# A selective-scan layer stage: a quarter of the B products on GpSimd, the skip term as a diagonal matmul, the gate on VectorE

## The chip, the cores and the metric

The kernel runs on one NeuronCore of a Trainium2 chip. The metric is the device time of one launch in microseconds, a median over runs. A core has a matrix engine (TensorE, in the profile PE, its weight loads PEld), three engines for elementwise work (VectorE = DVE, ScalarE = ACT, GpSimd = POOL) and SyncE (SP), which here only issues transfers. Each engine takes its instructions in the order in which they were written; they wait for one another by semaphores. TensorE writes to PSUM (eight banks of 128 x 512 fp32), the other data lie in SBUF.

## The reference

The network has four layers on an image x of shape (2, 128, 64, 64). Only the first, two rounds of a selective state-space block, is touched by the change. With `t` the tokens (2 images x 4096 positions, 128 channels), each round computes:

```python
xz = layernorm(t) @ in_w.T                     # u and z: 256 channels each
u  = silu(causal_conv4(u) + conv_b)
dt, Bm, Cm = split(u @ xproj_w.T, [8, 24])     # 8, 16 and 16 columns
dt = softplus(dt @ dt_w.T + dt_b)
dA = exp(dt[..., None] * A);  dBu = (dt * u)[..., None] * Bm[:, :, None, :]
h  = dA_t * h + dBu_t                          # scan over 4096 positions, 256 x 16 states
y  = einsum('bdn,bn->bd', h, C_t)
y  = (y + u * ssm_D) * silu(z)
t  = t + y @ out_w.T
t  = t + gelu(layernorm(t) @ w1.T + b1) @ w2.T + b2
```

Before the rounds stands a 1x1 embedding, behind them a 1x1 output projection and a residual. The later layers (two attention layers over 4096 positions, and a multi-scale layer) follow.

## The kernel before

The layer stage works on items: one image, one round, one chunk of CH = 512 positions, so 2 x 2 x 8 = 32 items. The states of an item are 256 channels x 16. They are laid out as NST = 8 groups; a group holds 32 channels x 4 state quarters on the 128 partitions, and in the free dimension m = 4 states of 512 positions. So one item has 32 slots, each one scan instruction of 128 x 512: slot t belongs to group g = t // 4, state m = t % 4.

All is written in one loop over slots, by hand; the order on each engine is the order written. For each slot the loop gives, in this order:

- at m = 0: `spread_dt` (SyncE copies 32 rows of dt to the four quarters of `dtb`, four transfers, for a group two ahead), `spread_dtu` (a TensorE matmul with a selection matrix puts dt*u of the next group on all quarters, into the PSUM tile `pdu`, which has one bank), and in odd groups `y_pair` (eight TensorE matmuls with a 128 x 32 selection sum h*C of two groups over the states into `py`, one bank);
- `scan` (VectorE, line 358): h = da * h + h along 512 positions, starting from `carry`. After m = 3 GpSimd saves the last column (line 360) and multiplies the group by C (line 361, 2048 elements a partition);
- `decay` (ScalarE, line 347): da = exp(A * dtb) for the slot four ahead, into one of four PSUM banks;
- at m = 3: `times_b` (VectorE, line 340): h of the next group = B * pdu, 2048 elements a partition;
- the background work of that slot, from a table in `background(i)`.

The background table spreads over the 32 slots of item i what its neighbours need: the item before it (p = i - 1) is finished, the next one (n = i + 1) gets its projections, i + 2 its first layer norm. The entries that matter here, by slot:

- 0 to 6: the convolution and z projections (`pu_taps`, `pz_mm`, each matmul followed by a ScalarE copy), gelu of item i - 2 (slot 3), `y_out` and `gate` of p (slot 6: VectorE forms y + D*u from PSUM, line 381; GpSimd multiplies by z, line 384), the second feed-forward matmuls (6 and 7);
- 8: `mix_out` (three matmuls, lines 390 and 391), 10: `mix_add` (ScalarE, line 394), 11: silu with two activation table loads;
- 12 to 15: layer-norm centring and squares; 13 and 14: `xproj` (B, C and the dt columns) and `spread_bc` (B and C go to DRAM, tile `dr`, and from there by eight transfers of 256 KB to `bb` and `cb`, two buffers each); 15 to 18: `dtproj`, softplus on ScalarE (line 315), `dt_end` (dt*u on GpSimd, line 321);
- 17 to 21: variance, inverse root, and one Newton step, `ln_newton` (line 226 on GpSimd, 227 on ScalarE) and `ln_step` (231 on GpSimd);
- 23: `y_out` of the item's first half; 27 to 29: the norm is spread (TensorE, line 235) and applied (VectorE, line 239); 30 and 31: the first feed-forward matmuls (line 403), into a tile `hid`.

The tiles h and hid rotate through one tag of five buffers. Small PSUM results share a tag of two banks, which ScalarE empties.

Of the kernel before, what the change touches and what calls it, by code (L numbers as in the profile page):

```python
# [6 lines left out]
F32 = mybir.dt.float32  # L7
AF = mybir.ActivationFunctionType
ALU = mybir.AluOpType
# [6 lines left out]
P = 128  # L16
CH = 512
# [3 lines left out]
DS = 16  # L21
DI = 2 * C
NJ = DI // P
R = (C + 15) // 16
NX = R + 2 * DS
KC = 4
# [41 lines left out]
def tile_conv_seq(ctx: ExitStack, tc, x, consts, vecs, wemb, wlay, wconv, wdt, wqkv, wsmall, wms, out):  # L68
# [30 lines left out]
    def v1(name, i=0):  # L99
        return vec[:, VEC[name] + i : VEC[name] + i + 1]  # L100
# [7 lines left out]
    with ExitStack() as s, tc.manual_schedule():  # L108
# [24 lines left out]
        wl, wu, wd, am = [], [], [], []  # L133
        for l in range(NL):
            w = wp.tile([P, NWL - DI], F32, name=f"wl{l}")
            nc.sync.dma_start(w, wlay[l][:, DI:])
            cw = sp.tile([P, KC + 1, DI], F32, name="cw", tag="h", bufs=5)
# [12 lines left out]
            for g in range(4):  # L150
                pa = mm.tile([P, NJ, DS], F32, name="pa", tag="mm")
                nc.tensor.matmul(pa.rearrange("p j n -> p (j n)"), lhsT=four(g), rhs=an, start=True, stop=True)
                for q in range(4):
                    at = slice(32 * q, 32 * q + 32)
                    nc.vector.tensor_copy(a[at, :, g, :], pa[at, :, 4 * q : 4 * q + 4])
            wl.append(w), wu.append(u), wd.append(d), am.append(a)
        for c in range(NCH):
            nc.sync.dma_start(xv(1, c), x[1, :, c * RPC : (c + 1) * RPC, :])
# [14 lines left out]
        def vl(name, i, k=0):  # L173
            return v1(f"{name}{items[i][1]}", k)
# [22 lines left out]

        def ln_square(w, k, i):
            if "sq" not in w:
                w["sq"] = sp.tile([P, 2, CH], F32, name="sq", tag="tmp", bufs=2)  # L200
# [39 lines left out]

        def ln_shift(w, k, i, second):
            if second:
                dst = st[i]["x2"] = sp.tile([P, CH], F32, name="x2", tag="tmp", bufs=2)
# [50 lines left out]
            st[i]["dbl"] = sp.tile([NX, CH], F32, name="dbl", tag="dbl")  # L294
            nc.scalar.copy(st[i]["dbl"], st[i].pop("pd"))

        def spread_bc(i):

            dr = dp.tile([2 * DS, CH], F32, name="dr", tag="dr")
            nc.sync.dma_start(dr, st[i]["dbl"][R:])  # L300
            for k in range(2):
                o = st[i]["bc", k] = sp.tile([P, 4, CH], F32, name=("bb", "cb")[k], tag=("bb", "cb")[k], bufs=2)
                for q in range(4):
                    src = dr[k * DS + 4 * q : k * DS + 4 * q + 4, :].rearrange("(o m) f -> o (m f)", o=1)
                    nc.sync.dma_start(o[32 * q : 32 * q + 32].rearrange("p m f -> p (m f)"), src.to_broadcast([32, 4 * CH]))

        def dtproj(i, j):
            st[i]["pt", j] = mmt("pt")
# [15 lines left out]
        def spread_dt(g):  # L324
            i, s_ = divmod(g, NST)
            o = st[i]["dtb", s_] = sp.tile([P, CH], F32, name="dtb", tag="dtb", bufs=4)
            k = 32 * (s_ % 4)
            for q in range(4):
                nc.sync.dma_start(o[32 * q : 32 * q + 32, :], st[i]["dt"][k : k + 32, s_ // 4, :])

        def spread_dtu(g):
            i, s_ = divmod(g, NST)
            pdu = st[i]["pdu", s_] = bc.tile([P, CH], F32, name="pdu", tag="bc")
            nc.tensor.matmul(pdu, lhsT=four(s_ % 4), rhs=st[i]["dtu"][:, s_ // 4, :], start=True, stop=True)  # L334

        def times_b(g):
            i, s_ = divmod(g, NST)
            h = st[i]["h", s_] = sp.tile([P, 4, CH], F32, name="h", tag="h", bufs=5)
            pdu = st[i].pop(("pdu", s_))
            nc.vector.tensor_tensor(h, st[i]["bc", 0], pdu.unsqueeze(1).to_broadcast([P, 4, CH]), ALU.mult)  # L340

        def decay(t):
            g, m = divmod(t, 4)
            i, s_ = divmod(g, NST)
            j, gg = divmod(s_, 4)
            da = st[i]["da", s_, m] = dap.tile([P, CH], F32, name="da", tag="da")
            nc.scalar.activation(da, st[i]["dtb", s_], AF.Exp, scale=am[items[i][1]][:, j, gg, m : m + 1])  # L347
# [15 lines left out]
        def y_pair(g):  # L363

            i, s_ = divmod(g, NST)
            j, gg = divmod(s_, 4)
            if gg == 0:
                st[i]["py", j] = yp.tile([P, CH], F32, name="py", tag="y")
            py = st[i]["py", j]
            for m in range(4):  # L370
                for k in range(2):
                    r = 32 * (gg + k)
                    nc.tensor.matmul(  # L373
                        py[r : r + 32, :], lhsT=sel, rhs=st[i]["h", s_ + k][:, m, :], start=(m == 0), stop=(m == 3),
                        tile_position=(0, r),
                    )


        def y_out(i, j):
            u = st[i]["u"][:, j, :]  # L380
            nc.vector.scalar_tensor_tensor(u, u, vl("ssm_D", i, j), st[i].pop(("py", j)), ALU.mult, ALU.add)

        def gate(i):
            nc.gpsimd.tensor_tensor(st[i]["z"], st[i]["z"], st[i]["u"], ALU.mult)

        def mix_out(i):
            po = st[i]["po"] = mmt("po")
# [9 lines left out]
        def ffn_up(i, f):  # L397
            w = st[i]
            if f == 0:
                w["hid"] = sp.tile([P, 4, CH], F32, name="hid", tag="h", bufs=5)  # L400
# [36 lines left out]
        def background(i):  # L437
# [3 lines left out]
            def at(t, f, *a):  # L441
                todo[t].append((f, a))
# [728 lines left out]
```

## Time and profile before

The time is 5351.36 us, the median of three runs (5349.31 to 5352.06). The profiled execution spans 5360.6 us.

| part of the span | us | what runs |
|---|---|---|
| layer stage, first to last scan | 83.5 to 2159.6 | 32 items of 32 slots |
| the layers behind it | to 5360.6 | attention and multi-scale layers |

| engine, whole span | busy us | share |
|---|---|---|
| PE | 4900.6 | 91% |
| DVE | 3798.2 | 71% |
| ACT | 2326.4 | 43% |
| POOL | 2287.5 | 43% |

How to read the profile: a group of instructions stands as line, engine, operation, output tile <- input tiles, shapes, count, then the busy time in us, the mean ns of one, and the idle time just before them with the instruction that ended most of it. A timeline line has the start, the length, the engine and the instruction, and in brackets the idle time before it with what ended it. In the list of waits, "A <- B: total, times, longest" says that A stood idle until B was done. One fp32 matmul shows as two records. Lines with "q" are the issuing of transfers or sequencer work.

### The profile page before, as it was taken

What the parts mean: (1) busy time and instruction counts of PE and PEld (TensorE: products, weight loads), DVE (VectorE), ACT (ScalarE), POOL (GpSimd) and SP (SyncE); (2) the same over time, 40 slices, a digit from 0 to 9 for tenths busy, and PEclk for the clock granted to TensorE, in tenths of its full rate; (3) what the DMA queues carried; (4) which work ended last, traced back from release to release, by engine and by line L of the source; (5) the groups of instructions that cost most, each with busy time, mean ns of one, the idle gap of its engine ahead of it and who ended that gap; (6) DMA issues with size and microseconds to landing.
All of it is one profiled execution on the core that took longest, in us unless ns stands there. A gap on an engine that the chain in (4) does not pass through costs nothing.

```text
span 5360.6 us, 48695 instructions
## 1 busy us (share of the span) xinstructions
PE 4900.6 (91%) x15085; PEld 2311.3 (43%) x15085; DVE 3798.2 (71%) x3810; ACT 2326.4 (43%) x2933; POOL 2287.5 (43%) x1948
## 2 busy tenths in 40 slices
PE   5888888888888898899999999999999998988997
PEld 1222222222222222356665566656666665333332
DVE  4998999889999999136663366667767775656665
ACT  4676777777777776212221122232323221223332
POOL 2766666666666767112221122223333332322221
PEclk8898889999898988899999999999999999999998
DMA  4222233222222232014442244444444442000000
GB/s 108 69 65 64 65 70 70 68 68 64 64 64 64 68 73 69 17 42 95 96 97 50 51 96 96 95 101 112 112 101 101 112 111 71 4 4 4 6 6 8
DMA packets 233843, 362.04 MB, mean 68 GB/s; under 512 B 87648, under 2 KB 88048, under 8 KB 225136
## 3 DMA queue, kind: packets, MB, share of 16 engines
q1 hardware_dynamic: 184432, 291.76, 23.2%
q10 hardware_dynamic: 49152, 67.17, 5.2%
q8 instruction: 121, 1.98, 0.2%
q14 instruction: 138, 1.13, 0.1%
HBM read 83.92 MB, written 6.29 MB: 17 GB/s over the span
## 4 chain that ended last, share of the span: by engine, by line
PE 59%; DVE 14%; DMA 10%; ACT 6%; SPq 4%; issue 4%; POOL 4%; ACTq 0%; DVEq 0%; POOLq 0%
PE pq L600 11%; PE po L647 11%; PE py L373 5%; PE pp L544 5%; DVE tr L627 4%; PE pu L262 4%; SPq L638 3%; DMA dtb<-dt 3%; DVE h L358 3%; DMA bb<-dr 3%; POOL h L361 3%; DMA pt<-tr 3%; PE pdu L334 2%; PE pf L861 2%; PE ph L403 2%
## 5 line engine op out<-in xcount | busy, mean ns | idle before, releaser
L634 POOL COPY pt<-tr 32x512 f32<-32x512 f32 x1024 | 628.0, 613 | 1680.7 <-DVE tr L627 911.8
L358 DVE TENSOR_TENSOR_SCAN h<-da,carry,h 128x512 f32<-128x512 f32 x1024 | 1240.2, 1267 | 97.6 <-ACT da L347 68.3
L361 POOL TENSOR_TENSOR h<-h,cb 128x2048 f32<-128x2048 f32 x256 | 1160.7, 4534 | 20.8 <-POOL carry L360 0.2
L604 DVE TENSOR_SCALAR_CACHE_REDUCE sc<-pq 128x1024 f32<-128x1024 f32 x512 | 625.9, 1223 | 760.6 <-PE pq L600 748.4
L647 PE MATMUL po<-pt,vt 128*128 128x256 f32 x4096 | 968.1, 380 | 4.8 <-DMA pt<-tr 4.8
L600 PE MATMUL pq<-k,q 128*128 128x512 f32 x2048 | 962.1, 592 | 4.8 <-ACT q L532 3.4
L647 PEld LDWEIGHTS po<-pt,vt 128*128 128x128 f32 x4096 | 776.4, 190 | 265.4 <-issue 170.6
L347 ACT ACTIVATE da<-dtb,am 128x512 f32<-128x512 f32 x1024 | 686.8, 685 | 390.3 <-DVE h L358 250.2
L613 ACT ACTIVATE sc<-sc,nm 128x4096 f32<-128x4096 f32 x128 | 474.8, 3709 | 721.9 <-DVE nm L611 615.6
L627 DVE STREAM_TRANSPOSE tr<-sc 128x2048 f32<-128x2048 f32 x256 | 589.3, 2302 | 37.9 <-DMA pt<-tr 24.5
L340 DVE TENSOR_TENSOR h<-bb,pdu 128x2048 f32<-128x2048 f32 x256 | 580.0, 2266 | 25.0 <-POOL carry L360 15.4
L373 PE MATMUL py<-h,sel 128*32 128x512 f32 x2048 | 506.7, 638 | 1.7 <-POOL h L361 1.7
L600 PEld LDWEIGHTS pq<-k,q 128*128 128x128 f32 x2048 | 383.5, 190 | 277.8 <-issue 248.7
L334 PE MATMUL pdu<-dtu,fsel 128*128 128x512 f32 x512 | 327.4, 726 | 87.8 <-DVE h L340 87.6
L532 ACT ACTIVATE q<-pqq,vec 128x256 f32<-128x256 f32 x64 | 30.4, 474 | 606.6 <-PE pqq L544 361.2
L373 PEld LDWEIGHTS py<-h,sel 128*32 128x32 f32 x2048 | 114.5, 117 | 412.5 <-issue 406.8
L544 PE MATMUL pp<-xt,wq 128*128 128x512 f32 x576 | 251.8, 598 | 6.6 <-DMA wq<-in_wqkv 6.2
L262 PE MATMUL pu<-xn,wu 128*128 128x512 f32 x512 | 246.1, 614 | 2.7 <-ACT xn L252 1.7
L235 PE MATMUL pr<-rs,kc 2*128 2x512 f32 (+1 forms) x128 | 117.1, 1059 | 133.1 <-POOL rs L231 126.9
L334 PEld LDWEIGHTS pdu<-dtu,fsel 128*128 128x128 f32 x512 | 95.2, 214 | 303.5 <-DVE h L340 187.9
L888 PE MATMUL pqkv<-f,ws 128*128 128x512 f32 x384 | 197.8, 641 | 10.2 <-ACT q L895 6.3
L950 DVE TENSOR_TENSOR ov<-v,pw 128x2048 f32<-128x2048 f32 x64 | 146.2, 2284 | 63.4 <-PE pw L943 63.3
(191 smaller groups left out, 5089.1 us busy)
## 6 DMA issues: line engine op xcount, KB each, us to landing
pt<-tr SPq DMA_DIRECT2D x2048, 64.0 KB, 2.0
dtb<-dt SPq DMA_DIRECT2D x1024, 64.0 KB, 2.0
pt<-tr ACTq DMA_DIRECT2D x1024, 64.0 KB, 2.1
bb<-dr SPq DMA_DIRECT2D x128, 256.0 KB, 4.5
cb<-dr SPq DMA_DIRECT2D x128, 256.0 KB, 7.6
xt<-in_x SPq DMA_DIRECT2D x16, 256.0 KB, 5.1
xr<-in_x SPq DMA_DIRECT2D x16, 256.0 KB, 3.1
out<-ot SPq DMA_DIRECT2D x16, 256.0 KB, 2.0
```

The costliest lines, as they stand in the source:

```text
L334: nc.tensor.matmul(pdu, lhsT=four(s_ % 4), rhs=st[i]["dtu"][:, s_ // 4, :], start=True, stop=True)
L340: nc.vector.tensor_tensor(h, st[i]["bc", 0], pdu.unsqueeze(1).to_broadcast([P, 4, CH]), ALU.mult)
L347: nc.scalar.activation(da, st[i]["dtb", s_], AF.Exp, scale=am[items[i][1]][:, j, gg, m : m + 1])
L358: nc.vector.tensor_tensor_scan(h[:, m, :], da, h[:, m, :], carries[b, l][:, j, gg, m : m + 1], ALU.mult, ALU.add)
L361: nc.gpsimd.tensor_tensor(h, h, st[i]["bc", 1], ALU.mult)
L373: nc.tensor.matmul(py[r : r + 32, :], lhsT=sel, rhs=st[i]["h", s_ + k][:, m, :], start=(m == 0), stop=(m == 3), tile_position=(0, r),)
L544: nc.tensor.matmul(ps, lhsT=wq[:, which, tap, :], rhs=rhs, start=(tap == 0), stop=(tap == 8))
L600: nc.tensor.matmul(pq[:, i, :], lhsT=st["q", r, grp][:, it * P : (it + 1) * P], rhs=st["k"][:, at : at + CH], start=True, stop=True)
L604: nc.vector.tensor_scalar(dst, pq, 1.0, None, ALU.mult, ALU.max, accum_out=st["mx"][:, c2 : c2 + 1])
L627: nc.vector.transpose(tr, half.rearrange("p (t r f) -> p r t f", r=NB, f=32))
L634: nc.gpsimd.tensor_copy(dst, src)
L647: nc.tensor.matmul(st["po", r, grp], lhsT=st["vt"][:, jt, :], rhs=rhs, start=(jt == 0), stop=(jt == N // P - 1))
```

## The change

It moves work of the scan loop among the engines, and reorders transfers:

- `times_b` keeps three of the four states on VectorE. The fourth is made by GpSimd (`times_b_last`, at m = 2, after the slot's background work). [...]ScalarE first copies pdu to SBUF (`copy_dtu`, at m = 1, tile `dub`, one buffer).
- The skip term D*u is no longer added by VectorE. A diagonal matrix `sd` of D, made in the setup, opens the accumulation of `py` with one more matmul for each half of an item.
- The gate, z*y, is one VectorE product that reads `py` from PSUM, for each half, at slots 7 and 23; the GpSimd product of the whole item goes. `mix_out` moves from slot 8 to 9.
- The transfers of C (slot 16) and of B (slot 27) are issued apart, and `bb` has one buffer in place of two; `spread_dt` runs three groups ahead in place of two.
- h and hid get six buffers in place of five; the tiles sq and x2 get a tag of their own.

```diff
-        def spread_bc(i):
-            for k in range(2):
-                o = st[i]["bc", k] = sp.tile([P, 4, CH], F32, name=("bb", "cb")[k], tag=("bb", "cb")[k], bufs=2)
+        def spread_bc(i, k):
+            o = st[i]["bc", k] = sp.tile([P, 4, CH], F32, name="bc"[k] + "b", tag="bc"[k] + "b", bufs=1 + k)
...
+        def copy_dtu(g):
+            o = st[i]["dub", s_] = sp.tile([P, CH], F32, name="dub", tag="dub")
+            nc.scalar.copy(o, st[i]["pdu", s_])
+        def times_b_last(g):
+            h = st[i]["h", s_] = sp.tile([P, 4, CH], F32, name="h", tag="h", bufs=6)
+            nc.gpsimd.tensor_tensor(h[:, 3, :], st[i]["bc", 0][:, 3, :], st[i].pop(("dub", s_)), ALU.mult)
         def times_b(g):
-            nc.vector.tensor_tensor(h, st[i]["bc", 0], pdu.unsqueeze(1).to_broadcast([P, 4, CH]), ALU.mult)
+            nc.vector.tensor_tensor(h[:, :3, :], st[i]["bc", 0][:, :3, :], pdu.unsqueeze(1).to_broadcast([P, 3, CH]), ALU.mult)
...
             if gg == 0:
-                st[i]["py", j] = yp.tile([P, CH], F32, name="py", tag="y")
+                py = st[i]["py", j] = yp.tile([P, CH], F32, name="py", tag="y")
+                nc.tensor.matmul(py, lhsT=skip[items[i][1]][:, j, :], rhs=st[i]["u"][:, j, :], start=True, stop=False)
...
-        def y_out(i, j):
-            nc.vector.scalar_tensor_tensor(u, u, vl("ssm_D", i, j), st[i].pop(("py", j)), ALU.mult, ALU.add)
-        def gate(i):
-            nc.gpsimd.tensor_tensor(st[i]["z"], st[i]["z"], st[i]["u"], ALU.mult)
+        def gate(i, j):
+            nc.vector.tensor_tensor(z, z, st[i].pop(("py", j)), ALU.mult)
...
-                at(6, y_out, p, 1), at(6, gate, p)
-                at(8, mix_out, p), at(10, mix_add, p)
+                at(7, gate, p, 1), at(9, mix_out, p), at(10, mix_add, p)
...
-                at(13, xproj, n), at(14, xproj_out, n), at(14, spread_bc, n)
+                at(13, xproj, n), at(14, xproj_out, n), at(14, store_bc, n), at(16, spread_bc, n, 1), at(27, spread_bc, n, 0)
...
-                at(23, y_out, i, 0)
+                at(23, gate, i, 0)
...
-                if m == 0 and 0 <= g + 2 < NG:
-                    spread_dt(g + 2)
+                if m == 0 and 0 <= g + 3 < NG:
+                    spread_dt(g + 3)
...
+                if m == 1 and 0 <= g + 1 < NG:
+                    copy_dtu(g + 1)
                 if m == 3 and 0 <= g + 1 < NG:
                     times_b(g + 1)
                 for f, a in todo[t_]:
                     f(*a)
+                if m == 2 and 0 <= g + 1 < NG:
+                    times_b_last(g + 1)
```

More of the change, by code (lines that the diff above doesn't have):

```diff
@@ L132, in tile_conv_seq @@
         nc.scalar.preload_act_table_set(EXP_LN_SET)
-        wl, wu, wd, am = [], [], [], []
+        wl, wu, wd, am, skip = [], [], [], [], []
         for l in range(NL):
@@ L136, in tile_conv_seq @@
             nc.sync.dma_start(w, wlay[l][:, DI:])
-            cw = sp.tile([P, KC + 1, DI], F32, name="cw", tag="h", bufs=5)
+            cw = sp.tile([P, KC + 1, DI], F32, name="cw", tag="h", bufs=6)
             nc.sync.dma_start(cw[:, :KC, :].rearrange("p k d -> p (k d)"), wconv[l : l + 1, :].to_broadcast([P, KC * DI]))
@@ L155, in tile_conv_seq @@
                     nc.vector.tensor_copy(a[at, :, g, :], pa[at, :, 4 * q : 4 * q + 4])
+            sd = wp.tile([P, NJ, P], F32, name=f"sd{l}")
+            for j in range(NJ):
+                nc.vector.tensor_scalar(sd[:, j, :], ident, v1(f"ssm_D{l}", j), None, ALU.mult)
+            skip.append(sd)
             wl.append(w), wu.append(u), wd.append(d), am.append(a)
@@ L199, in ln_square @@
             if "sq" not in w:
-                w["sq"] = sp.tile([P, 2, CH], F32, name="sq", tag="tmp", bufs=2)
+                w["sq"] = sp.tile([P, 2, CH], F32, name="sq", tag="sq")
                 w["cen"] = sp.tile([P, 2, CH], F32, name="cen", tag="cen")
@@ L242, in ln_shift @@
             if second:
-                dst = st[i]["x2"] = sp.tile([P, CH], F32, name="x2", tag="tmp", bufs=2)
+                dst = st[i]["x2"] = sp.tile([P, CH], F32, name="x2", tag="x2")
             else:
@@ L295, in xproj_out, with store_bc @@
             nc.scalar.copy(st[i]["dbl"], st[i].pop("pd"))
-        def spread_bc(i):
-            dr = dp.tile([2 * DS, CH], F32, name="dr", tag="dr")
-            nc.sync.dma_start(dr, st[i]["dbl"][R:])
-            for k in range(2):
-                o = st[i]["bc", k] = sp.tile([P, 4, CH], F32, name=("bb", "cb")[k], tag=("bb", "cb")[k], bufs=2)
-                for q in range(4):
-                    src = dr[k * DS + 4 * q : k * DS + 4 * q + 4, :].rearrange("(o m) f -> o (m f)", o=1)
-                    nc.sync.dma_start(o[32 * q : 32 * q + 32].rearrange("p m f -> p (m f)"), src.to_broadcast([32, 4 * CH]))
+        def store_bc(i):
+            st[i]["dr"] = dp.tile([2 * DS, CH], F32, name="dr", tag="dr")
+            nc.sync.dma_start(st[i]["dr"], st[i]["dbl"][R:])
+        def spread_bc(i, k):
+            o = st[i]["bc", k] = sp.tile([P, 4, CH], F32, name="bc"[k] + "b", tag="bc"[k] + "b", bufs=1 + k)
+            for q in range(4):
+                src = st[i]["dr"][k * DS + 4 * q : k * DS + 4 * q + 4, :].rearrange("(o m) f -> o (m f)", o=1)
+                nc.sync.dma_start(o[32 * q : 32 * q + 32].rearrange("p m f -> p (m f)"), src.to_broadcast([32, 4 * CH]))
         def dtproj(i, j):
@@ L334, in spread_dtu @@
             nc.tensor.matmul(pdu, lhsT=four(s_ % 4), rhs=st[i]["dtu"][:, s_ // 4, :], start=True, stop=True)
+        def copy_dtu(g):
+            i, s_ = divmod(g, NST)
+            o = st[i]["dub", s_] = sp.tile([P, CH], F32, name="dub", tag="dub")
+            nc.scalar.copy(o, st[i]["pdu", s_])
+        def times_b_last(g):
+            i, s_ = divmod(g, NST)
+            h = st[i]["h", s_] = sp.tile([P, 4, CH], F32, name="h", tag="h", bufs=6)
+            nc.gpsimd.tensor_tensor(h[:, 3, :], st[i]["bc", 0][:, 3, :], st[i].pop(("dub", s_)), ALU.mult)
         def times_b(g):
             i, s_ = divmod(g, NST)
-            h = st[i]["h", s_] = sp.tile([P, 4, CH], F32, name="h", tag="h", bufs=5)
+            h = st[i]["h", s_]
             pdu = st[i].pop(("pdu", s_))
-            nc.vector.tensor_tensor(h, st[i]["bc", 0], pdu.unsqueeze(1).to_broadcast([P, 4, CH]), ALU.mult)
+            nc.vector.tensor_tensor(h[:, :3, :], st[i]["bc", 0][:, :3, :], pdu.unsqueeze(1).to_broadcast([P, 3, CH]), ALU.mult)
         def decay(t):
@@ L373, in y_pair @@
                     nc.tensor.matmul(
-                        py[r : r + 32, :], lhsT=sel, rhs=st[i]["h", s_ + k][:, m, :], start=(m == 0), stop=(m == 3),
+                        py[r : r + 32, :], lhsT=sel, rhs=st[i]["h", s_ + k][:, m, :], start=False, stop=(m == 3),
                         tile_position=(0, r),
                     )
-        def y_out(i, j):
-            u = st[i]["u"][:, j, :]
-            nc.vector.scalar_tensor_tensor(u, u, vl("ssm_D", i, j), st[i].pop(("py", j)), ALU.mult, ALU.add)
-        def gate(i):
-            nc.gpsimd.tensor_tensor(st[i]["z"], st[i]["z"], st[i]["u"], ALU.mult)
+        def gate(i, j):
+            z = st[i]["z"][:, j, :]
+            nc.vector.tensor_tensor(z, z, st[i].pop(("py", j)), ALU.mult)
         def mix_out(i):
@@ L399, in ffn_up @@
             if f == 0:
-                w["hid"] = sp.tile([P, 4, CH], F32, name="hid", tag="h", bufs=5)
+                w["hid"] = sp.tile([P, 4, CH], F32, name="hid", tag="h", bufs=6)
             ph = mmt("ph")
```

## The prediction

> **What bounds the kernel now.** I read the busy windows first, then the costliest groups, the list of waits for 1000 to 2000 us, and last the timelines of the engines over one period of the layer stage. The change touches that stage alone: the scan rows run from 83.5 to 2159.6 us, 32 items, so 64.9 us an item.
>
> ```profile
> 83.00:2160.00 2077.00, 1825.31 (x4593) 556.40 (x4594) 1879.33 (x1404) 1464.02 (x2073) 1425.95 (x669) 0.89 0.29 67
> ```
>
> (Columns: window, length, busy us of PE, PEld, DVE, ACT, POOL, clock, DMA share, GB/s.) Per item: VectorE 58.7 us, TensorE 57.0, ScalarE 45.8, GpSimd 44.6. No engine is full, so the period is set by a chain that passes from one to another.
>
> ```profile
> L358 DVE TENSOR_TENSOR_SCAN h<-da,carry,h 128x512 f32<-128x512 f32 x1024 | 1240.2, 1267 | 97.6 <-ACT da L347 68.3
> L361 POOL TENSOR_TENSOR h<-h,cb 128x2048 f32<-128x2048 f32 x256 | 1160.7, 4534 | 20.8 <-POOL carry L360 0.2
> L340 DVE TENSOR_TENSOR h<-bb,pdu 128x2048 f32<-128x2048 f32 x256 | 580.0, 2266 | 25.0 <-POOL carry L360 15.4
> ```
>
> (The costliest groups: busy us, mean ns, idle before.) And the waits of 1000 to 2000 us, total, times and longest:
>
> ```profile
> POOL dtu L321 <- ACT dt L315: 73.7, 15, 5.7
> ...
> ACT da L347 <- DMA dtb<-dt: 61.6, 15, 5.0
> ...
> DVE u L381 <- PE py L373: 38.9, 25, 2.2
> ...
> ACT xt L394 <- PE po L391: 32.9, 16, 2.1
> ```
>
> Fifteen or sixteen times in 1000 us, so once an item: ScalarE waits for TensorE (L394), GpSimd for ScalarE (dtu), ScalarE for a transfer (dtb). One period, in the timelines of ScalarE, GpSimd and TensorE (start us, length), shows how they hang together.
>
> ```profile
> 1282.06 0.59 ACT L394 COPY xt<-po 128x512 f32<-128x512 f32 x1 [2.05 <-PE po L391]
> ...
> 1306.74 0.69 ACT L347 ACTIVATE da<-dtb,am 128x512 f32<-128x512 f32 x1 [4.29 <-DMA dtb<-dt]
> 1307.37 0.70 ACT L227 ACTIVATE nt<-nt,c 2x512 f32<-2x512 f32 x1
> 1307.98 3.89 ACT L347 ACTIVATE da<-dtb,am 128x512 f32<-128x512 f32 x6
> ...
> 1346.95 0.59 ACT L394 COPY xt<-po 128x512 f32<-128x512 f32 x1 [2.05 <-PE po L391]
> ```
>
> ```profile
> 1297.26 2.35 POOL L321 TENSOR_TENSOR dtu<-dt,u 128x1024 f32<-128x1024 f32 x1 [4.86 <-ACT dt L315]
> 1299.55 0.18 POOL L360 COPY carry<-h 128x4 f32<-128x4 f32 x1
> ...
> 1304.33 1.26 POOL L226 TENSOR_TENSOR nt<-nt,ve 2x512 f32<-2x512 f32 x1
> ```
>
> ```profile
> 1314.55 2.07 PE L334 MATMUL pdu<-dtu,fsel 128*128 128x512 f32 x2 [1.31 <-DVE h L340]
> ...
> 1344.18 1.88 PE L390 MATMUL po<-z,wl 128*128 128x512 f32 x4
> 1345.89 1.02 PE L391 MATMUL po<-xt,kc 128*128 128x512 f32 x2
> ```
>
> Three stretches follow each other:
> **C**, from L394 (slot 10) to dtu: 1282.06 to 1297.26 = 15.20 us. ScalarE has no gap in it: silu with two table loads, the decays, the squares, softplus.
> **A**, from dtu to the pdu of slot 28: 1297.26 to 1314.55 = 17.29 us. ScalarE stands 4.29 us at the decay whose dtb came behind the B and C spreads in SyncE's queue; then VectorE does four scans and a B product, and frees pdu's only bank.
> **B**, from that pdu to the next L394: 1314.55 to 1346.95 = 32.40 us. TensorE runs without a gap through 2 y pairs, 4 pdu, 4 ph, 8 pu, 2 pz, 5 pf and 3 po, to the po on which L394 waits.
> They sum to 64.89. Over eight periods each that I read the means are 15.0, 17.3 and 32.8, so this one is typical. VectorE and GpSimd have slack in B and C.
>
> **What the Trainium skill says.** GPSIMD Engine Reference, Elementwise side-by-side: a two-input fp32 tensor_tensor of 2048 costs 4497 ns on GpSimd and 2293 on VectorE; the trace agrees (4534 and 2266). The same page, Specifications: GpSimd shares its SBUF interface with VectorE, and they contend where VectorE's instruction has two SBUF inputs or a 2-port mode. Every L361 here takes 4507 to 4569 ns beside scans and products that read one operand from PSUM; the new VectorE products also read one from PSUM, so I keep GpSimd's times. TensorE: Matmul & The Clock Gate, opening table: the other compute engines are strict first-in first-out, which the 4.29 us above agrees with (L227 stood behind a decay). The same page, What's actually happening: after an idle window TensorE runs at half rate; the pdu of slot 28 agrees, 2.07 us for a record pair that later takes 1.02.
>
> **The change, part by part.**
> VectorE: the B product loses a quarter, 8 x about 0.53 us (2266/2048 ns an element, 512 of them, less its fixed share) = 4.3 us an item; y_out (0.75) becomes a gate from PSUM. A 128x512 product with a PSUM operand isn't in this stage; between 0.57 (a quarter of L340) and 0.75 (L381), I take 0.66. VectorE falls from 58.7 to about 54. It isn't the bound, so this pays only where VectorE lies on the chain: the one product in A.
> GpSimd: eight products of 512 added, 1.25 us each by the 2x512 row L226, gate of 2.36 removed: 44.6 + 10 - 2.4 = 52 us. Full at 80%, but one of the eight, emitted in slot 18, stands between dtu and nt, and ScalarE's L227 waits for nt with the next decay behind it: that one is on the chain. Its own wait is for copy_dtu, which ScalarE issues before softplus, so it is ready.
> ScalarE: eight copies of pdu, 0.59 alone (L204), 0.48 in a row. Those of slots 13 and 17 lie in C, which is gapless: on the chain. In B ScalarE waits for TensorE anyway, which hides three; those of slots 21, 25 and 29 come after the decay that VectorE needs. dub has one buffer, so a copy also waits for GpSimd's product of the group before; that product ran a group earlier (behind the copy stand the decays, which are four slots ahead of the scans).
> TensorE: two skip matmuls, 0.86 each (1344.18 to 1345.89 is 1.71 for two). That of slot 28 lies in B: on the chain. That of slot 12 lies in C, where TensorE is some 0.9 to 1.3 us ahead of ScalarE at pc and pd: hidden by ScalarE.
> Transfers: dtb three groups ahead, cb alone at slot 16, bb at slot 27. The 4.29 us wait goes.
> The y_out wait of 2.16 us at slot 6 goes by moving to slot 7, but VectorE has slack in B.
> bb with one buffer is a new wait: SyncE holds the load until VectorE's product of slot 27 and GpSimd's of slot 26 have read it; behind it are only dtb loads that have two groups to spare. The last of four issues starts 1.3 us after the first and lands in 4.4 (median for bb, cb queued behind): 5.7 to 7.5 us. VectorE's product of slot 31 and GpSimd's of slot 30 wait for it.
> py, six h buffers, own tags for sq and x2, and the skip weights, made once in the setup with four small VectorE products: nothing on the chain. The first and last items run with partly empty queues; I give them the same change as the others.
>
> **The sum.** New A: dtu 2.29, the product 1.22 (L226 less overlap), carry and h*cb 4.78 (1299.55 to 1304.33), nt and the handover 1.33, L227 to the decay 0.61, decay to scan 0.73 (1306.74 to 1307.47), three scans 3.54 (slot 24's is already done), B product to pdu 2.32 - 0.53 = 1.79. Together 16.29: 1.00 less than 17.29. The removed transfer wait uncovers the GpSimd chain, which has just grown.
> New B: 32.40 + 0.86 = 33.26. bb: GpSimd's product of slot 26 ends dtu + 18.9, bb lands at 24.6 to 26.4, VectorE's product ends 1.75 later, 26.4 to 28.2; TensorE wants that bank at 16.29 + 10.05 + 0.86 = 27.2. I take it as just hidden, with up to 1.0 exposed as the bound.
> New C: 15.20 + 2 x 0.49 = 16.18.
> 65.73 against 64.89 is +0.84 an item, x 32 = +27 us: 5351 + 27 = 5378. The stages behind aren't touched.
>
> **Rivals.**
> R1, VectorE is the bound: 8 x 0.53 and two gates at 0.09 less, 4.4 us an item, come straight off, with or without the 2.16 us wait at slot 6; x 32 = -141 to -210, so 5141 to 5210, say 5190. For it: its 90% share. Against it: L394's and dtu's waits don't name it.
> R2, the transfer wait counts and the additions hide: A falls by 1.0 (1.2 more without the GpSimd product), B and C stay: -1.0 to -2.2 x 32, about 5305. For it: the wait comes in every period. Against it: C is gapless on ScalarE and B on TensorE.
> R3, bb's load, or GpSimd's new lateness, shows in B: 1 to 1.5 us more an item: about 5420. For it: margins of under 1 us.
>
> **How the numbers follow.** Forecast 0.49, R1 0.10, R2 0.20, R3 0.21. The forecast's own spread, half a microsecond an item (16 us), puts 0.37 of it beyond +0.2% and 0.12 within. Faster: R1 and R2, 0.30. Slower: 0.37 + 0.21 = 0.58. Range 5280 to 5440: it holds R2 and R3 and leaves out R1 and the tails.
>
> **What would show it.** Right: ScalarE's wait for dtb gone; L394 still waiting for po; dtu to pdu about 16.3, pdu to L394 about 33.3, L394 to dtu about 16.2; VectorE idle more than before. Wrong: an item below 64, or L394 no longer waiting (R1, R2); long waits of VectorE or TensorE behind bb (R3).

## The result and the profile after

The changed kernel takes **5512.7 us**, the median of four runs (5511.0 to 5518.0), against 5351.2 (5349.3 to 5352.1) for the kernel before on the same chip: a ratio of 1.0303, interval 1.0288 to 1.0318. It is slower, as forecast, but by 161 us, not by the 27 of the forecast, and outside the range given. The loss lies in the layer stage: behind its last scan the profiled executions take 3199.8 us before and 3196.3 after.

The window over the layer stage shows an item at (2311.6 - 84.0) / 32 = 69.6 us in place of 64.9. The busy windows' row of the changed kernel, columns as in the prediction:

```profile
83.00:2320.00 2237.00, 1933.92 (x4740) 597.97 (x4741) 1745.69 (x1404) 1602.22 (x2332) 1673.84 (x897) 0.87 0.27 62
```

Per item VectorE is busy for 54.6 us and GpSimd for 52.3, as worked out (54 and 52), ScalarE for 50.1 and TensorE for 60.4. So the work was moved as meant, and the engines' sums don't explain the loss: VectorE has 4 us less to do, and is idle for 69.6 - 54.6 = 15.0 us an item where it was 64.9 - 58.7 = 6.2. The costliest groups say in front of what:

```profile
L374 DVE TENSOR_TENSOR_SCAN h<-da,carry,h 128x512 f32<-128x512 f32 x1024 | 1237.2, 1265 | 35.3 <-ACT da L363 14.2
L377 POOL TENSOR_TENSOR h<-h,cb 128x2048 f32<-128x2048 f32 x256 | 1159.0, 4528 | 20.6
...
L356 DVE TENSOR_TENSOR h<-bb,pdu 128x1536 f32<-128x1536 f32 x256 | 446.8, 1745 | 452.0 <-ACT dub L345 418.3
...
L339 PE MATMUL pdu<-dtu,fsel 128*128 128x512 f32 x512 | 350.3, 772 | 231.6 <-DVE h L356 231.6
L350 POOL TENSOR_TENSOR h<-bb,dub 128x512 f32<-128x512 f32 x256 | 330.1, 1290 | 448.5 <-ACT dub L345 317.2
```

The end of the L356 row is the news: VectorE's B product, which had 25 us of idle time before it in the kernel before, now has 452, and 418 of them end with ScalarE's copy of pdu (L345). VectorE does not read that copy; only GpSimd does. And TensorE's pdu matmul has 231.6 us behind L356. The list of waits for 1000 to 2000 us gives the counts:

```profile
DVE h L356 <- ACT dub L345: 195.8, 64, 6.5
...
POOL h L350 <- ACT dub L345: 152.7, 52, 4.7
...
PE pdu L339 <- DVE h L356: 95.4, 28, 6.1
...
ACT nt L231 <- POOL nt L230: 44.7, 14, 4.0
...
ACT xt L408 <- PE po L405: 11.4, 15, 0.8
```

ScalarE's wait for dtb is all but gone (2.4 us, once), L408 (the old L394) still waits for po, and VectorE waits for the copy 64 times, 4.5 times an item, up to 6.5 us. In the three stretches of the forecast (A from dtu to the pdu of slot 28, B from there to mix_add, C from there to dtu), as means over some 27 periods:

| stretch | before | forecast | after |
|---|---|---|---|
| A | 17.34 | 16.29 | 20.19 |
| B | 32.75 | 33.26 | 33.71 |
| C | 15.11 | 16.18 | 16.37 |

B and C are near the forecast. A was to fall and rose: 3.90 more than forecast, x 32 = 125 us, most of the 135 us that the forecast missed. One period, in the timelines of the changed kernel, shows A. ScalarE first:

```profile
1322.11 0.72 ACT L231 ACTIVATE nt<-nt,c 2x512 f32<-2x512 f32 x1 [3.96 <-POOL nt L230]
1322.74 0.67 ACT L363 ACTIVATE da<-dtb,am 128x512 f32<-128x512 f32 x1
1323.35 0.57 ACT L345 COPY dub<-pdu 128x512 f32<-128x512 f32 x1
```

GpSimd, on which L231 waits:

```profile
1312.54 2.34 POOL L326 TENSOR_TENSOR dtu<-dt,u 128x1024 f32<-128x1024 f32 x1 [2.48 <-ACT dt L320]
1314.84 1.29 POOL L350 TENSOR_TENSOR h<-bb,dub 128x512 f32<-128x512 f32 x1
1316.06 0.20 POOL L376 COPY carry<-h 128x4 f32<-128x4 f32 x1
1316.34 4.52 POOL L377 TENSOR_TENSOR h<-h,cb 128x2048 f32<-128x2048 f32 x1
1320.82 1.25 POOL L230 TENSOR_TENSOR nt<-nt,ve 2x512 f32<-2x512 f32 x1
```

VectorE, and TensorE behind it:

```profile
1316.16 1.28 DVE L374 TENSOR_TENSOR_SCAN h<-da,carry,h 128x512 f32<-128x512 f32 x1 [0.27 <-POOL h L350]
1323.95 1.75 DVE L356 TENSOR_TENSOR h<-bb,pdu 128x1536 f32<-128x1536 f32 x1 [6.51 <-ACT dub L345]
1325.62 0.68 DVE L398 TENSOR_TENSOR z<-z,py 128x512 f32<-128x512 f32 x1
1326.22 4.80 DVE L374 TENSOR_TENSOR_SCAN h<-da,carry,h 128x512 f32<-128x512 f32 x4
1330.94 1.73 DVE L356 TENSOR_TENSOR h<-bb,pdu 128x1536 f32<-128x1536 f32 x1
```

```profile
1325.76 2.07 PE L339 MATMUL pdu<-dtu,fsel 128*128 128x512 f32 x2 [5.74 <-DVE h L356]
...
1332.72 2.08 PE L339 MATMUL pdu<-dtu,fsel 128*128 128x512 f32 x2 [1.18 <-DVE h L356]
```

Read it from ScalarE's 1322.11. L231, the half of the Newton step, stands at the head of the queue for 3.96 us, because GpSimd reaches nt only after dtu, its new quarter, the carry and the product with C. Behind L231 stand a decay and then the copy of slot 21. VectorE finished a scan at 1317.44 and stood until 1323.95, 0.03 us after the end of the copy. Then a B product, a gate and four scans still lay ahead of the product that frees pdu for slot 28.

Why does VectorE wait for a copy it does not read? Both instructions read pdu, one PSUM bank. The Trainium skill ("PSUM — Partial Sum Buffer", section "PSUM bank collisions raise a hardware error") says that two engines may not access one bank in the same partitions at once, reads against reads included, and that software has to keep them apart; the program orders the two reads with a semaphore, the copy first since it was written first. The trace agrees with that: of the 256 products of L356 and the 256 copies of L345 in the layer stage, no two overlap in time, while in run e8 below, where the copy reads SBUF in place of the bank, 63 of the 256 copies overlap such a product. No run here lets two engines read one bank at once, so what that would do is not shown.

### The profile page after: what moved, and what is told of

Its sections match the earlier page's. It is cut to its first block, busy times and chain, and to the rows that moved or that the text cites. A ratio compares the mean times of both kernels' runs of the same rounds, so it can differ in the third digit from the quotient of the medians.

```text
span 5509.1 us, 49238 instructions
## 1 busy us (share of the span) xinstructions
PE 4997.4 (91%) x15213; PEld 2350.5 (43%) x15213; DVE 3663.5 (66%) x3814; ACT 2459.7 (45%) x3189; POOL 2530.6 (46%) x2172
## 4 chain that ended last, share of the span: by engine, by line
PE 61%; DVE 15%; ACT 7%; POOL 6%; SPq 4%; DMA 3%; issue 3%; ACTq 0%; DVEq 0%; POOLq 0%
PE pq L617 11%; PE po L664 11%; PE py L390 5%; PE pp L561 5%; DVE h L374 4%; DVE tr L644 4%; PE pu L266 4%; SPq L655 3%; POOL h L377 3%; DVE h L356 3%; PE pdu L339 3%; PE pf L878 2%; DMA pt<-tr 2%; PE pf L429 2%; PE ph L417 2%
## 5 line engine op out<-in xcount | busy, mean ns | idle before, releaser
L377 POOL TENSOR_TENSOR h<-h,cb 128x2048 f32<-128x2048 f32 x256 | 1159.0, 4528 | 20.6
L356 DVE TENSOR_TENSOR h<-bb,pdu 128x1536 f32<-128x1536 f32 x256 | 446.8, 1745 | 452.0 <-ACT dub L345 418.3
L339 PE MATMUL pdu<-dtu,fsel 128*128 128x512 f32 x512 | 350.3, 772 | 231.6 <-DVE h L356 231.6
L350 POOL TENSOR_TENSOR h<-bb,dub 128x512 f32<-128x512 f32 x256 | 330.1, 1290 | 448.5 <-ACT dub L345 317.2
L390 PE MATMUL py<-h,sel 128*32 128x512 f32 x2048 | 486.2, 617 | 2.8 <-POOL h L377 2.8
L971 POOL TENSOR_TENSOR ov<-ov 128x2048 f32<-128x2048 f32 x16 | 72.7, 4542 | 255.8 <-DVE ov L967 255.8
```

The source lines that it names most:

```text
L356: nc.vector.tensor_tensor(h[:, :3, :], st[i]["bc", 0][:, :3, :], pdu.unsqueeze(1).to_broadcast([P, 3, CH]), ALU.mult)
L377: nc.gpsimd.tensor_tensor(h, h, st[i]["bc", 1], ALU.mult)
L390: nc.tensor.matmul(py[r : r + 32, :], lhsT=sel, rhs=st[i]["h", s_ + k][:, m, :], start=False, stop=(m == 3), tile_position=(0, r),)
```

## The experiments

The theory: the copy of slot 21, kept from running by the Newton half ahead of it, holds VectorE by the shared bank, and that is the +3.9 us of A. Rivals: the additions as such (more work on GpSimd, ScalarE and TensorE), the skip term and the gate, and bb's single buffer. All runs, in stretches and as ratios to the kernel before on the same chip:

| run | A | B | C | us | ratio (interval) |
|---|---|---|---|---|---|
| after | 20.19 | 33.71 | 16.37 | 5512.7 | 1.0303 (1.0288 to 1.0318) |
| e1 copy at m = 0 | 16.25 | 35.20 | 17.18 | 5456.0 | 1.0190 (1.0175 to 1.0205) |
| e2 no share | 15.66 | 33.93 | 15.48 | 5350.6 | 0.9990 (0.9982 to 0.9999) |
| e3 no skip | 20.25 | 33.03 | 16.30 | 5494.2 | 1.0259 (1.0244 to 1.0275) |
| e4 transfers only | 16.05 | 33.32 | 15.10 | 5338.8 | 0.9961 (0.9947 to 0.9975) |
| e5 skip only | 17.44 | 33.74 | 15.45 | 5391.5 | 1.0068 (1.0053 to 1.0083) |
| e6 lighter chain | 15.06 | 31.21 | 15.37 | 5245.6 | 0.9795 (0.9780 to 0.9810) |
| e7 Newton half later | 16.43 | 34.80 | 16.36 | 5424.0 | 1.0128 (1.0113 to 1.0144) |
| e8 copy from SBUF | 16.26 | 34.73 | 16.28 | 5420.0 | 1.0123 (1.0106 to 1.0140) |
| e10 as e8, two bb | 16.25 | 34.05 | 16.28 | 5385.7 | 1.0047 (1.0031 to 1.0064) |
| e11 as e7, two bb | 16.46 | 33.83 | 16.36 | 5392.9 | 1.0061 (1.0046 to 1.0076) |

(A, B, C are means over the steady periods; the first and last items run with other lengths, so 32 times a sum does not give the time to the microsecond. e10 and e11 ran on another chip than e1 to e8, so they are compared with these by the ratios.)

**Which part costs: e2, e3, e4, e5.** e2 is the changed kernel without the share: no copy, and VectorE makes all four states.

```diff
-            nc.vector.tensor_tensor(h[:, :3, :], st[i]["bc", 0][:, :3, :], pdu.unsqueeze(1).to_broadcast([P, 3, CH]), ALU.mult)
+            nc.vector.tensor_tensor(h, st[i]["bc", 0], pdu.unsqueeze(1).to_broadcast([P, 4, CH]), ALU.mult)
...
-                if m == 1 and 0 <= g + 1 < NG:
-                    copy_dtu(g + 1)
...
-                if m == 2 and 0 <= g + 1 < NG:
-                    times_b_last(g + 1)
```

> The changed kernel without GpSimd's quarter and without the copy: VectorE makes all four states of a product; skip matmul, gate and transfers as changed. T1: A is the chain without wait and without the extra product, about 15.6; B about 33.7 by the skip matmul, C back to 15.1: 64.4 an item, about 5330, under the kernel before. T2 with bb's single buffer as the cause: stays above 5450. If the skip matmul and the new transfer order were the cost, it would also stay there.

It came to 0.9990: the share costs 5512.7 - 5350.6 = 162 us, the whole loss, and the rest of the change sums to nothing. A is 15.66, so with the transfer wait gone and no new product on GpSimd, A falls by 1.7; B takes back 1.2 and C 0.4.

e3 is the changed kernel with the skip term and the gate of the kernel before (`y_out` on VectorE at slots 6 and 23, `gate` on GpSimd, `mix_out` at 8).

```diff
-                nc.tensor.matmul(py, lhsT=skip[items[i][1]][:, j, :], rhs=st[i]["u"][:, j, :], start=True, stop=False)
...
-                at(7, gate, p, 1), at(9, mix_out, p), at(10, mix_add, p)
+                at(6, y_out, p, 1), at(6, gate, p), at(8, mix_out, p), at(10, mix_add, p)
```

> The changed kernel without the skip matmul and with the old y_out on VectorE and gate on GpSimd. T1: A and C as in the changed kernel (20.2, 16.4), B shorter by the skip matmul's 0.86: about 5485. A theory that puts the loss on the diagonal matmul and the gate expects about 5350.

A stays at 20.25 and B falls by 0.68: the skip term lengthens B, as forecast, and has no part in A's rise. e5 does the reverse, the skip term and the gate alone on the kernel before:

```diff
+                nc.tensor.matmul(py, lhsT=skip[items[i][1]][:, j, :], rhs=st[i]["u"][:, j, :], start=True, stop=False)
...
-                at(6, y_out, p, 1), at(6, gate, p)
-                at(8, mix_out, p), at(10, mix_add, p)
+                at(7, gate, p, 1)
+                at(9, mix_out, p), at(10, mix_add, p)
```

> The kernel before with the skip matmul, the gate on VectorE and mix_out at slot 9, nothing else. By the prediction's step: B longer by 0.86 us, A and C as before, +27 us, near 5380. If TensorE isn't the bound of B: 5351 or less, since VectorE and GpSimd lose work.

B rose by 1.0, C by 0.34 and A by 0.1, and the time by 0.68%, 36 us. The forecast had 0.86 in B for that matmul, and nothing in C.

e4 has the transfers alone on the kernel before: C and B issued apart at slots 16 and 27, one bb, dtb three groups ahead.

```diff
-                at(13, xproj, n), at(14, xproj_out, n), at(14, spread_bc, n)
+                at(13, xproj, n), at(14, xproj_out, n), at(14, store_bc, n), at(16, spread_bc, n, 1), at(27, spread_bc, n, 0)
...
-                if m == 0 and 0 <= g + 2 < NG:
-                    spread_dt(g + 2)
+                if m == 0 and 0 <= g + 3 < NG:
+                    spread_dt(g + 3)
```

> The kernel before with the transfers alone changed: C at slot 16, B at slot 27 with one buffer, dtb three groups ahead. If the removed dtb wait counts by the prediction's sum: A from 17.3 to 15.6, B and C unchanged (32.7, 15.1), 52 us less, about 5300. If the single buffer of B costs more than the wait saves: above 5351.

Less than half of what was expected: 0.39%, about 21 us in place of 52. A fell by 1.29 and not by 1.7, and B rose by 0.57. The timelines show where. In the kernel before, VectorE's `y_out` of slot 23 waited for an unfinished y pair, and behind it VectorE still stood for the late decay, so `y_out` cost nothing:

```profile
1304.87 0.75 DVE L381 SCALAR_TENSOR_TENSOR u<-u,vec,py 128x512 f32<-128x512 f32 x1 [0.81 <-PE py L373]
1307.47 4.85 DVE L358 TENSOR_TENSOR_SCAN h<-da,carry,h 128x512 f32<-128x512 f32 x4 [1.85 <-ACT da L347]
```

In e4 it waits as long, but the four scans follow it at once, so it now lies on the chain:

```profile
1418.14 0.75 DVE L382 SCALAR_TENSOR_TENSOR u<-u,vec,py 128x512 f32<-128x512 f32 x1 [0.81 <-PE py L374]
1418.80 4.80 DVE L359 TENSOR_TENSOR_SCAN h<-da,carry,h 128x512 f32<-128x512 f32 x4
```

B grows at its start, on TensorE. The pdu that opens B takes 2.07 us and the y pair behind it 5.37, where an earlier y pair of the same period took 3.63:

```profile
1414.44 3.63 PE L374 MATMUL py<-h,sel 128*32 128x512 f32 x16
...
1425.84 2.07 PE L335 MATMUL pdu<-dtu,fsel 128*128 128x512 f32 x2 [3.12 <-DVE h L341]
1427.84 5.37 PE L374 MATMUL py<-h,sel 128*32 128x512 f32 x16
```

The clock granted to TensorE, which the profile records as a share of its full speed (the third number from the end in a row of busy windows), is 0.67 over that y pair; over the y pair in the same place of the kernel before, which takes 4.39 us, it is 0.82:

```profile
1427.84:1433.21 5.37, 5.37 (x18) 1.22 (x17) 4.17 (x4) 2.58 (x5) 2.76 (x4) 0.67 1.02 213
```

```profile
1316.55:1320.94 4.39, 4.39 (x18) 1.01 (x17) 4.17 (x4) 2.58 (x5) 2.60 (x3) 0.82 0.06 15
```

As means over 27 periods this y pair takes 4.71 us before and 5.27 in e4, and the rest of B behind it 26.1 in both, so it is the whole rise of B. The single bb buffer is not: VectorE waits for it 2.1 us in 1000.

**Whether it is the copy, and by what: e1, e7, e8.** e1 moves the copy one slot up, directly behind the matmul that makes pdu, and so ahead of the Newton half.

```diff
                 if m == 0 and 0 <= g + 1 < NG:
                     spread_dtu(g + 1)
+                    copy_dtu(g + 1)
...
-                if m == 1 and 0 <= g + 1 < NG:
-                    copy_dtu(g + 1)
```

> As the changed kernel, but ScalarE copies pdu right behind its matmul, at m = 0, ahead of L227 (the Newton step) and softplus in ScalarE's order. T1 (VectorE's B product waits for ScalarE's copy because both read the one PSUM bank, and the copy of slot 21 stands behind L227): stretch A falls from 20.2 us to about 16.3, as in the prediction's sum; B and C stay at 33.7 and 16.4, so about 125 us less, near 5388. T2 (the lateness comes from GpSimd's own product, in front of nt and hcb, or from the single buffer of bb): A stays near 20 and the time near 5510.

A fell to 16.25, close to the forecast's 16.29, but the time only to 1.019: at its new place the copy itself waits for TensorE, in front of mix_add and the decays, and for GpSimd, since dub has one buffer. Four lines of its list of waits, where L345 has become a waiter:

```profile
DVE h L356 <- ACT dub L345: 85.4, 54, 3.1
ACT dub L345 <- PE pdu L339: 77.2, 43, 3.9
...
ACT dub L345 <- POOL h L350: 56.4, 30, 3.0
...
DVE h L356 <- DMA bb<-dr: 42.6, 12, 3.8
```

The copy of slot 8 waits 3.9 us ahead of mix_add, and C goes to 17.2 and B to 35.2. So e1 shows where A's time was, but is no clean test of the gain.

e7 leaves the copy and moves the Newton half one slot later (slot 21, behind the copy; `ln_step` to 22).

```diff
+        def ln_half(w, n):
+            nt = w["nt"][:n]
             nc.scalar.activation(nt, nt, AF.Identity, bias=c15[:n], scale=-0.5)
...
-                at(20, ln_newton, w, m), at(21, ln_step, w, m)
+                at(20, ln_newton, w, m), at(21, ln_half, w, m), at(22, ln_step, w, m)
```

> The changed kernel with the bank still shared, but ScalarE's half of the Newton step (L227 before, L231 after) written at slot 21, behind the decay and the copy of that slot, and rs at slot 22. T1: the copy no longer stands behind a wait for GpSimd, VectorE's product of slot 23 goes 4 us earlier, A near 16.3, the time near 5390 as in the run that reads SBUF. If the bank wait costs wherever the copy stands: well above 5390.

A is 16.43 and C as in the changed kernel; 89 us went, where A's fall alone would give 120. VectorE's wait for the copy at slot 23 is still there, but 2.2 us as a mean where the changed kernel has 6.0. e8 keeps every instruction where the changed kernel has it, and lets the copy read another tile of the same shape, in SBUF; so GpSimd's quarter of h is B * dt in place of B * dt * u there.

```diff
-            nc.scalar.copy(o, st[i]["pdu", s_])
+            nc.scalar.copy(o, st[i]["dtb", s_])
```

> The changed kernel, with ScalarE's copy at its place but reading another tile: dtb in SBUF in place of pdu in PSUM. It changes the computation: GpSimd's quarter of h is B*dt, not B*dt*u. All instructions, sizes and their order stay; only the one PSUM bank is no longer read by two engines. T1 (VectorE's product waits for the copy because of the bank): A falls from 20.2 to 16.3 us, B and C stay near 33.7 and 16.4, about 5390. T2 (ScalarE's extra work or GpSimd's extra product is the cost, not the bank): stays at 5510.

This one separates the bank from the copy's work, place and readers. (The copy also no longer waits for the pdu matmul, but at slot 21 it did not wait for it in the changed kernel either: it follows the decay without a gap.) Its list of waits has no line of L356 behind L345 any more, while the copy still runs late and GpSimd still waits for it:

```profile
POOL h L350 <- ACT dub L345: 139.1, 34, 7.4
...
DVE h L356 <- DMA bb<-dr: 45.8, 13, 3.8
```

and in its timeline the B product of slot 23 follows the scan at once; the decay of slot 21, three scans and the product that frees pdu come later:

```profile
1404.43 1.28 DVE L374 TENSOR_TENSOR_SCAN h<-da,carry,h 128x512 f32<-128x512 f32 x1 [1.12 <-ACT da L363]
1405.63 1.73 DVE L356 TENSOR_TENSOR h<-bb,pdu 128x1536 f32<-128x1536 f32 x1
...
1410.97 3.63 DVE L374 TENSOR_TENSOR_SCAN h<-da,carry,h 128x512 f32<-128x512 f32 x3 [1.39 <-ACT da L363]
1414.52 1.73 DVE L356 TENSOR_TENSOR h<-bb,pdu 128x1536 f32<-128x1536 f32 x1
```

A lies between 16.23 and 16.29 in every period. Together with e7, which keeps the shared bank and takes away what held the copy back, it shows the cause of A's extra length: VectorE's product ordered behind the late copy of the same bank.

**What takes part of it back: e10, e11.** In e1, e7 and e8 A is 3.7 to 3.9 us shorter than in the changed kernel, which would be 120 us, and the time fell by only 57 to 93. B had risen by 1.0 to 1.5, and the bb line of e8's list points to the single bb buffer: with A short, VectorE reaches the next item's first B product before bb has landed. A short A alone doesn't do it: e2 has 15.66 and one buffer too, and waits for bb 12.3 us in 1000, where e8 waits 45.8. In e2 the load goes out 15.6 us after dtu, when VectorE's product of slot 27 has read the buffer; in e8 at 18.9, when GpSimd's new product of slot 26 has. e10 and e11 are e8 and e7 with two buffers for bb, its transfers at slot 22 in place of 27, and five buffers for h and hid to make room.

```diff
-            o = st[i]["bc", k] = sp.tile([P, 4, CH], F32, name="bc"[k] + "b", tag="bc"[k] + "b", bufs=1 + k)
+            o = st[i]["bc", k] = sp.tile([P, 4, CH], F32, name="bc"[k] + "b", tag="bc"[k] + "b", bufs=2)
...
-                at(16, spread_bc, n, 1), at(27, spread_bc, n, 0)
+                at(16, spread_bc, n, 1), at(22, spread_bc, n, 0)
```

> e8 with two buffers for bb, its four transfers issued at slot 22 in place of 27, and five buffers for h and hid in place of six (the memory for the second bb). As in e8 GpSimd's quarter of h is B*dt in place of B*dt*u. Theory (with A short, the single bb buffer is what keeps B long: VectorE waits up to 3.8 us for it and TensorE's pdu behind it): no wait of line 356 for bb, A 16.3, B back to about 33.3, C 16.3, so 65.9 us an item against e8's 66.7; 0.8 x 32 = 26 us below e8, about 5394, ratio to the kernel before 1.006. Rival 1 (the bb wait falls into VectorE's slack, and B is long for TensorE's cold clock or the period near 40): the wait goes and the time stays at e8's ratio, 1.012. Rival 2 (five h buffers bring a wait of GpSimd's product or of the feed-forward's hid): a ratio of 1.015 or more.

> e7 (the changed kernel with the half of the Newton step one slot later, so that copy_dtu of slot 21 stands ahead of it) with two buffers for bb, its transfers at slot 22 and five buffers for h and hid. All of the reference is computed. Theory: as e10, A 16.5, B about 33.4, C 16.4, so 66.3 against e7's 67.2 and 0.8 x 32 = 26 us below e7: about 5398, ratio 1.007. Rival 1 (bb's wait is hidden anyway): e7's ratio, 1.013. Rival 2 (five h buffers cost): 1.016 or more.

Both came out a little better than the theory's figure: 1.0047 and 1.0061. The two buffers and the earlier slot were changed together, and no run parts them. The waits for bb are gone from their lists, and the median B fell from 34.17 to 33.48 and from 34.03 to 33.36, near the theory's 33.3 and 33.4 (the means stay higher, mostly for the three long periods under "Open"). e11 still lets ScalarE and VectorE read pdu's bank, and its list of waits still has the wait for the copy:

```profile
POOL h L353 <- ACT dub L348: 152.8, 51, 4.7
DVE h L359 <- ACT dub L348: 139.6, 60, 4.1
```

That is 139.6 us in 1000, against 195.8 in the changed kernel, and yet A, the median B and C are within 0.2 us of what the forecast gave them without any such wait. So most of these waits must lie where VectorE has slack; the dear one was that of slot 23, in A, here 2.2 us in place of 6.0.

**A version that beats both: e6.** If the three stretches are in series, the time falls only when one of them gets shorter. e6 takes the transfers of e4, the later Newton half of e7, moves `y_out` of slot 23 to 27, behind A, and takes the two z projections of the next item out of B into slots 24 to 26, where TensorE stood waiting for VectorE. No share, no skip matmul.

```diff
-                at(1, pz_mm, i, 0), at(3, pz_out, i, 0)
-                at(5, pz_mm, i, 1), at(6, pz_out, i, 1)
+                at(24, pz_mm, n, 0), at(25, pz_out, n, 0)
+                at(25, pz_mm, n, 1), at(26, pz_out, n, 1)
...
-                at(20, ln_newton, w, m), at(21, ln_step, w, m)
+                at(20, ln_newton, w, m), at(21, ln_half, w, m), at(22, ln_step, w, m)
...
-                at(23, y_out, i, 0)
+                at(27, y_out, i, 0)
```

> The transfers' new order alone, and three moves by the theory of the three stretches: ScalarE's half of the Newton step behind the next decay (slot 21, rs at 22), y_out of the first half from slot 23 to 27, and the two z projections of an item, with their copies, in slots 24 to 26 of the period before, where TensorE idles, in place of slots 1 to 6. If A, B and C are a chain in series: A from 16.1 to about 14.9, B from 33.3 to about 31.6 (two matmuls at 0.86), C 15.1: about 90 us under the run with the transfers alone, near 5250. If another engine bounds the item: no more than the transfers alone gave, near 5340.

It takes 5245.6 us, ratio 0.9795 (0.9780 to 0.9810). The three moves were made together, and no run parts them. A is 15.06 and B 31.21, 1.5 below the kernel before. TensorE's timeline in e6 shows where the z projections went, between the last pdu of A and the one that opens B:

```profile
1421.08 1.13 PE L338 MATMUL pdu<-dtu,fsel 128*128 128x512 f32 x2 [0.19 <-DVE h L344]
1422.04 1.88 PE L278 MATMUL pz<-xn,wl 128*128 128x512 f32 x4
...
1428.50 2.08 PE L338 MATMUL pdu<-dtu,fsel 128*128 128x512 f32 x2
```

B is 33.32 - 31.21 = 2.11 below e4's; the two matmuls (four records) that left it were worth 1.71 at the 0.86 each of the forecast. VectorE, the busiest engine of the stage, does the same work in e6 as before (1873 us of busy time against 1879).

## Why the forecast was wrong

**What held.** The reading of the period as three stretches in series, none set by an engine's total, fits all runs, though the stretches are not independent: in e1 and e4 a shorter A came with a longer B. The direction was right, but 2.85 of the growth of an item is A's, which was to fall; e11 (1.0061) shows that the change is slower without that too. R1 (VectorE is the bound) is out: with 4 us less of work on it the item grew. ScalarE's wait for dtb went, and the chain behind it, on GpSimd, is what A then hangs on: from dtu to the decay the forecast had 10.23 us, and the timeline has 1322.74 - 1312.54 = 10.20. The durations were good too: 1.745 us for the product of three states (2.27 - 0.53 = 1.74 in the forecast), 0.68 for the gate (0.66), 1.29 for GpSimd's quarter (1.25), 0.58 for the copy (0.59). L377 kept its 4.53 us.

**The step that failed.** It is the sentence on ScalarE: "those of slots 21, 25 and 29 come after the decay that VectorE needs". That made the copy of slot 21 free. It does come behind the decay, but VectorE needs the copy itself, since the B product of slot 23 waits for it at the shared bank. So the sum of A, which went on from the decay with 0.73 to the scan and "three scans 3.54 (slot 24's is already done)", left out what now stood there. In the trace, from that decay's start to the first of the scans it is 1326.22 - 1322.74 = 3.48 us and not 0.73 (the copy, a B product of 1.75 and a gate of 0.68 lie between): 2.75 more. There are four scans, at 1330.94 - 1326.22 = 4.72 and not 3.54: 1.18 more. Together 3.93, the miss in A. e8, which takes away that one shared read, e7, which takes away what held the copy back, and e1 all bring A back to 16.25 to 16.43. In the period of e8 shown above even the parts of the sum come out: 10.20 from dtu to the decay, 0.70 to the scan, 3.55 for three scans and 1.78 to pdu, against 10.23, 0.73, 3.54 and 1.79.

The sign of the miss was there to be read before: pdu has one bank, VectorE read it, and the change gave it a second reader. The forecast asked of that reader when it is issued and what it waits for, and not who must wait for it.

**B and C: close, in B by luck.** B rose by 0.96 against 0.86 forecast. But the 0.86 is the price of the skip matmul at full clock, and where it opens the y pairs of B the granted clock is 0.50: the changed kernel's timeline has

```profile
1334.59 1.92 PE L385 MATMUL py<-u,sd 128*128 128x512 f32 x2
1336.43 3.88 PE L390 MATMUL py<-h,sel 128*32 128x512 f32 x16
```

As means, the y pair starts 1.62 us later after pdu than in the kernel before and takes 0.59 less, as the clock over it is higher (0.93 in this period, 0.82 in the one of the kernel before). The two errors nearly cancel. C rose by 1.26 against 0.98. The share accounts for 0.9 to 1.2 of it (the changed kernel against e2, e3 against e4; two copies of 0.58 are 1.16); the skip term, put at nothing there, adds 0.34 when it stands alone (e5) and 0.07 beside the share (e3).

**R3 came second.** bb's load was taken as "just hidden, with up to 1.0 exposed as the bound". In the changed kernel A's extra 3.9 us hide most of it: VectorE waits for bb 8.2 us in 1000, against 45.8 in e8. Once A has its forecast length, bb is exposed. In e8 it lands 25.8 us after dtu as a mean, inside the forecast's 24.6 to 26.4 (the page before has 4.5 us as its median landing, where the forecast read 4.4); e10 and e11 take 0.7 off the median B, inside that bound, and 0.76% and 0.67% off the time, some 41 and 36 us. Both repairs together, e11, give A 16.46, median B 33.36 and C 16.36, against 16.29, 33.26 and 16.18; its ratio of 1.0061 is 33 us above the kernel before, where the forecast had 27. So the forecast described the change without the long wait at the bank and with bb in time.

**R2, its gain.** The transfers alone (e4) are worth 0.4%, about 21 us, not the 46 of R2, because B takes back 0.57 of the 1.29 an item that A saves.

**Open.** In e7 and e8 every eighth period, at the change of image or round, has a B of 39 to 40 us, in e1 of 40 to 41, and in e10 and e11 of 36 to 39; the longest in the kernel before is 33.8 and in the changed kernel 35.6. Three such periods are some 16 us of e8's time. VectorE's timeline in one of them (e8) has two waits, one behind the other:

```profile
1151.81 1.75 DVE L356 TENSOR_TENSOR h<-bb,pdu 128x1536 f32<-128x1536 f32 x1 [3.64 <-DMA bb<-dr]
1158.08 4.81 DVE L374 TENSOR_TENSOR_SCAN h<-da,carry,h 128x512 f32<-128x512 f32 x4 [4.52 <-POOL carry L372]
```

L372 sets carry to zero for a new sequence, on GpSimd, and stands there behind the new product and the product with C. VectorE waits for it three times in the stage, 1.9 us each in the kernel before and 4.4 in the changed one. No run moved it, so what it is worth is open.

## What to carry to other kernels

When a change gives a buffer a second reader on another engine, price the wait between the two readers and not only the wait for the writer: where the program keeps the two reads of a PSUM bank apart, as here, the later reader inherits everything that stands in the earlier reader's queue. e7 put the other reader where nothing ahead of it waits long; to put the reader on the critical path first is the other way, and no run here tried it. And moving work off the busiest engine pays only if a stretch of the chain loses an instruction by it; here one of the eight quarters taken from VectorE lay on the chain, for 0.53 us by the forecast's price, while e8 against e2, with the bank's wait in neither, still has A longer by 16.26 - 15.66 = 0.6 and C by 16.28 - 15.48 = 0.8 us.

## What the runs showed of the hardware

The clock granted to TensorE at the start of B was a larger term than expected. The pdu that opens B ran at 0.50 of full speed in the kernel before and in e4, 2.07 us for a pair that later takes 1.02. The y pair behind it took 4.39 us at 0.82 and 5.37 at 0.67, against 3.63 earlier in the period of e4, where the granted clock was 1.00. As means TensorE stood 1.45 us ahead of that pdu in the kernel before and 2.92 in e4. That the longer stand keeps the clock low for longer, so that e4 gave back in B part of what it saved in A, is argued and not shown: no run changed the wait alone, and in e6, where this wait is 0.13 us, the y pair still took 5.02. The forecast's sums kept TensorE's durations in B fixed.
